# A two-layer graph attention kernel: another order of products, copies and side work where one block of queries follows the last

## The chip, the cores and the metric

The kernel runs on one NeuronCore of a Trainium2 chip. Five engines work side by side, each through its own list of instructions in order: TensorE (PE, matrix products into PSUM), VectorE (DVE), ScalarE (ACT, here almost only exponentials), GpSimd (POOL, which here works in SBUF alone) and SyncE (SP, which here only issues transfers). An instruction that must wait for another engine holds up everything behind it on its own engine. The metric is device time in microseconds (us) of one execution; lower is better.

## The reference

There are 3327 nodes with 128 features and a dense 0/1 matrix `adj` of 3327 x 3327. Cut to what matters:

```python
# layer 0: graph attention over the neighbours
H = x @ W.T + b;  s = H @ a_s;  r = H @ a_r
e = leaky_relu(A * s + A * r.T, 0.2)
x = layernorm(x + softmax(where(A > 0, e, NEG), axis=1) @ H)
# layer 1: attention in 128 slices of 8 channels, adj added twice to the scores
q = (x @ Wq.T).reshape(128, n, 8)      # k and v alike
a = softmax(einsum('dnh,dmh->dnm', q, k) * 128 ** -0.5 + adj + adj, axis=2)
out = einsum('dnm,dmh->dnh', a, v).reshape(n, 1024)
x = layernorm(x + out @ Wo.T)
```

Layer 1 is nearly all of the work: 128 matrices of 3327 x 3327 scores, each with its exponential, and products with only 8 channels on either side. The kernel takes no maximum in its softmax (a flag computed on the way tells whether that is safe, and a general program stands behind it for other inputs).

## The kernel before, in words

**The main loop (L1126 to L1187).** The 128 slices are taken in 32 groups of 4. The 3327 queries of a group are taken in 7 blocks of 476 (the last one a little narrower), and the 3327 keys in 26 tiles of up to 128. That makes 224 blocks. One block is 26 *rounds*, so there are 5824 rounds. A round makes the scores of one key tile for four slices, as two halves of two slices. For each half (128 keys x 2 x 476 queries):

- PE multiplies keys by queries (L152, `scb`) into a PSUM tile of two banks.
- The `adj` term gets in by one of two ways. In an *add* tile, DVE adds `adj` to the scores (L1175) and writes to SBUF, and ACT takes the exponential of both halves at once, 1904 wide, one round later (`exp_late`, L991: the *late* exponential). In a *times* tile, ACT takes the exponential straight from PSUM, 952 wide (L1172: the *direct* one), and POOL multiplies it by a factor 1 + (e^2 - 1) adj (L1173).
- PE multiplies the result `e` by the values (`products`, L950; the products are L956) and sums over the 26 key tiles in one PSUM bank `av`. After the last tile DVE copies `av` to SBUF (L966) and SP writes it out.

Key tiles come in threes: one times tile i and two add tiles i+1, i+2. `laid` (L927) writes out the three rounds of a three: direct half 1 of i with add half 0 of i+1; direct half 0 of i with add half 1 of i+1; both add halves of i+2. An even block has eight threes and then two rounds with tile 24 (times) and tile 25 (add). An odd block starts with one round of tile 25 (add), then eight threes (rounds 1 to 24), then a round in which tile 24 is half direct and half add. Even and odd blocks alternate. By *passage* I mean the last rounds of a block with the first rounds of the next.

**Buffers.** Scores for adds have two PSUM tiles (`pd`, L920), scores for direct exponentials one (`pe`, L921), `av` one (`pv`, L922), and the side work one bank.[...] `e` has seven SBUF tiles.

**When the products run.** `multiply` (L977) appends the round's tile to a list and, at the end of the round, runs products while more than `LAG` = 4 tiles wait: one tile's four products per round, four rounds after its turn. So a block's last products run at the end of round 3 of the next block, the copy of `av` follows on DVE, and the first products of the new block (round 4) wait for that copy. In odd blocks the products and copy of round 3 stand between the two adds of that round (`between`, L1162).

**Side work.** Layer 0 for the 26 tiles of rows, the projections to q, k and v, the counting of `adj` (L326, a part of the flag) and the results of layer 1 (`result`, L482) are cut into small pieces that run between rounds. A piece has a letter: `p` runs on PE at the head of a round (side products are L241, transposes L376 and L502), `d` on DVE at its end, `l` (the low halves, L409) on DVE as well, `m` on POOL (weights of layer 0: `weigh`, L308, and `mask`, L317), `x` issues transfers. Pieces wait in two rows, `main` and `aside`; `n` and `t` entries make a piece wait for a mark that another one sets. `lane` and `reading` (L1007 to L1017) say in which rounds a letter may run: `p`, `d` and `m` in round 0 and 25 of even blocks, in round 25 of odd ones, and in every third round between; `p` also in round 3 (4 in odd blocks). The counts stand in `aside`, behind the weights. `finish_to` (L1108) runs what is still missing when a new group needs its rows.

Of the kernel before, what the change touches and what calls it, by code (L numbers as in the profile page):

```python
# [17 lines left out]
P = 128  # L18
# [29 lines left out]
def kernel(  # L48
# [29 lines left out]
    H = wqT.shape[1]  # L78
# [71 lines left out]
    def special():  # L150
# [9 lines left out]
        with ExitStack() as sx, tc.manual_schedule(engines=ALL):  # L160
# [9 lines left out]
            CH = [(i, min(i + CW, NT)) for i in range(0, NT, CW)]  # L170
# [96 lines left out]
            def layer0(t, side=True, trow=None, bank=bank, held=None):  # L267
# [5 lines left out]
                s = {"a": {}, "w": {}}  # L273
                q0 = t * len(CH)
# [190 lines left out]
                for n, (i0, i1) in enumerate(CH):  # L465

                    aside.append(("n", ("P", q0 + n - 2, 0)))
                    for c0 in range(i0, i1, 3):
                        c1 = min(c0 + 3, i1)
                        aside.append(("m", lambda n=n, c0=c0, c1=c1: weigh(n, c0, c1)))  # L470
                        aside.append(("m", lambda n=n, c0=c0, c1=c1: mask(n, c0, c1)))
                    aside.append(("t", ("W", q0 + n)))
                    c = [("d", lambda n=n, h=h, k=k: count(n, h, k)) for h in range(3) for k in range(2)]
                    counts.append(c)
                    main.append(("n", ("W", q0 + n, 3)))
                    if i1 == NT:
                        main.append(("m", biased))
                    main += [("p", lambda i=i: product(i)) for i in range(i0, i1)] + [("t", ("P", q0 + n))]
                    aside.append(counts[-1])
                return loads, main + chain + [("t", ("rows", t))], aside  # L480

            def result(t):  # L482
# [440 lines left out]
            LAG = 4  # L923
# [90 lines left out]
            def lane(kind, n, odd):  # L1014

                if kind == "l":
                    return int(reading(n - 1, odd) if n else True)  # L1017
                return int(reading(n, odd) or kind == "p" and n - odd == 3)

            made = [layer0(t) for t in range(1, NT)]  # L1020
            first_loads = made[0][0]
            main = []
            aside = []
            for n, (_, m, a) in enumerate(made):

                later = []
                for u in a:
                    if u[0] == "r":

                        at = max((k for k, v in enumerate(aside) if v[0] == "n"), default=0)  # L1030
# [8 lines left out]
                if n == 0:  # L1039

                    for k, u in enumerate(later):
                        aside += u + [made[1][0][k]] * (len(made) > 1)
                main.append(m)
            main.append([("n", ("counts", 0, 0))] + judge())
            aside.append(("t", ("counts", 0)))
# [3 lines left out]
            side = {"main": [], "aside": aside, "since": {"main": 0, "aside": 0}, "read": -2}  # L1049

            def head(row, now, force=False):

                while True:
                    if not side[row]:
                        if row == "aside":
# [24 lines left out]

            def work_tensor(now, n, odd):

                for _ in range(lane("p", n, odd) if side["read"] != now - 1 else 0):
                    if head("main", now) != "p":
                        break
                    run("main", now)

            def work(now, n, odd):
                room, low, pool = lane("d", n, odd), lane("l", n, odd), lane("m", n, odd)
                for row in ("main", "aside"):  # L1090
                    while True:
                        kind = head(row, now)
                        if kind == "x":
# [13 lines left out]

            def finish_to(mark, now):  # L1108
                while mark not in marks:
                    row = "main" if head("main", -1 if now is None else now, True) else "aside"  # L1110
                    if head(row, -1 if now is None else now, True) is None:
                        break
                    run(row, -1)
                    tick(True)
# [13 lines left out]
            for g in range(NG):  # L1128
                k4, v4, _ = group
                for b in range(NBLK):  # L1130
# [5 lines left out]
                    for n, rnd in enumerate(rounds):  # L1136
# [437 lines left out]
```

## Time and profile before

| | |
|---|---|
| Time, median of 3 runs | 10047.45 us (10043.44 to 10048.37) |
| The profiled execution: time | 10052.42 us |
| The profiled execution: span of its instructions | 10050.6 us |
| Granted TensorE clock | 0.995 |
| ACT busy | 9897.6 us, 98% of the span |
| PE busy | 9477.4 us, 94% |
| DVE busy | 9188.5 us, 91% |
| POOL busy | 9177.2 us, 91% |
| DMA | mean 175 GB/s |

Times in the profile's timeline are microseconds from the start of the span. A timeline row has the start, the time over which the row's instructions ran, engine, line, operation, output<-input with shape and how many (x), and in brackets how long the engine was idle before and what ended that. "PEld" is the loading of weights for a product. The busy time of a matrix product is modelled, and instructions of one engine overlap in the records[...]. So the distance from one start to the next tells more of an engine's pace than the length of a row.

### The profile page before, as it was taken

Reading aid. Unit: us, or ns where it says so; the run is one execution under the profiler, and the core shown is the slowest. Engines: PE = TensorE matmul, PEld = TensorE weight load, DVE = VectorE, ACT = ScalarE, POOL = GpSimd, SP = SyncE. Lnnn points to the kernel's source line nnn. Section 1 sums busy time; section 2 is a strip of 40 time slices with the busy share of each in tenths; the row PEclk is TensorE's granted clock in tenths of the full one; section 3 lists DMA queues with packets and bytes.
Section 4 is the critical chain, followed back from the end, with each engine's and each line's share of the span. In section 5 each row is a group of like instructions: output and inputs, shape, how many; then the busy total and the mean of one; then the engine's idle time right before and its main releaser. Section 6 shows DMA issues by size and latency. Waiting matters only on the chain.

```text
span 10050.6 us, 207550 instructions
## 1 busy us (share of the span) xinstructions
PE 9477.4 (94%) x79523; PEld 3013.9 (30%) x79523; DVE 9188.5 (91%) x10554; ACT 9897.6 (98%) x7904; POOL 9177.2 (91%) x4954
## 2 busy tenths in 40 slices
PE   7999999999999999999999999999999999999998
PEld 2233333333233233323333333333333233222222
DVE  7899999999999999999999999999999999888888
ACT  7999999999999999999999999999999999999998
POOL 7999999999999999999999999999999999888887
PEclk9999999999999999999999999999999999999999
DMA  6765656665665656565566656566665565555554
GB/s 194 209 179 179 179 168 183 178 176 168 181 173 171 183 167 189 168 184 170 169 179 187 176 172 179 176 170 178 181 179 175 171 175 168 169 158 166 164 164 132
DMA packets 1399414, 1755.28 MB, mean 175 GB/s; under 512 B 349360, under 2 KB 1386890, under 8 KB 1394312
## 3 DMA queue, kind: packets, MB, share of 16 engines
q1 hardware_dynamic: 1388061, 1739.30, 59.7%
q8 instruction: 626, 10.26, 0.4%
q10 hardware_dynamic: 10347, 2.61, 0.1%
q14 instruction: 380, 3.11, 0.1%
HBM read 1637.49 MB, written 103.93 MB: 173 GB/s over the span
## 4 chain that ended last, share of the span: by engine, by line
ACT 41%; PE 21%; POOL 16%; issue 13%; DVE 7%; DMA 2%; SPq 1%; POOLq 0%; ACTq 0%; DVEq 0%
ACT e L991 29%; POOL e L1173 15%; ACT e L1172 11%; PE av L956 11%; PE scb L152 9%; DVE e L1175 5%; PE bank L241 1%; DVE o L966 1%; DMA q4b<-qT 1%; DMA at<-in_adjT_dram 1%; POOL w L308 0%; SPq L733 0%; POOL w L317 0%; DMA k4b<-kT 0%; POOL at L793 0%
## 5 line engine op out<-in xcount | busy, mean ns | idle before, releaser
L1173 POOL TENSOR_TENSOR e<-e,at 128x952 f32<-128x952 f32 (+1 forms) x3920 | 8715.9, 2236 | 788.6 <-ACT e L1172 735.1
L1175 DVE TENSOR_TENSOR e<-scb,at 128x952 f32<-128x952 f32 (+1 forms) x7728 | 8499.4, 1142 | 769.7 <-PE scb L152 650.1
L991 ACT ACTIVATE e<-e 128x1904 f32<-128x1904 f32 (+3 forms) x3920 | 7095.9, 1810 | 26.4 <-DVE e L1175 11.1
L956 PE MATMUL av<-e,v4b 128*32 128x476 f32 (+1 forms) x46592 | 5843.8, 573 | 99.0 <-DVE o L966 68.0
L152 PE MATMUL scb<-q4b,k4b 32*128 32x476 f32 (+1 forms) x23296 | 3882.4, 486 | 440.8 <-ACT e L1172 361.9
L1172 ACT ACTIVATE e<-scb 128x952 f32<-128x952 f32 (+1 forms) x3920 | 3921.1, 1000 | 74.9 <-PE scb L152 36.7
L152 PEld LDWEIGHTS scb<-q4b,k4b 32*128 32x128 f32 (+1 forms) x23296 | 1779.3, 189 | 5459.2 <-ACT e L1172 3161.5
L956 PEld LDWEIGHTS av<-e,v4b 128*32 128x32 f32 (+1 forms) x46592 | 1014.1, 109 | 1239.9 <-issue 933.4
L241 PE MATMUL bank<-hsb,w 128*32 128x129 f32 (+1 forms) x5200 | 278.6, 286 | 0.0
L326 DVE TENSOR_SCALAR_CACHE_REDUCE dump<-a 128x384 bf16<-128x384 f32 (+2 forms) x468 | 247.3, 528 | 0.6
L308 POOL TENSOR_SCALAR w<-trow,er 128x129 f32<-128x129 f32 x650 | 231.6, 376 | 1.3
L317 POOL TENSOR_TENSOR w<-w,a 128x384 f32<-128x384 f32 (+3 forms) x225 | 207.9, 924 | 0.1
L966 DVE COPY o<-av 128x476 f32<-128x476 f32 (+1 forms) x224 | 145.2, 648 | 31.3 <-PE av L956 30.4
L241 PEld LDWEIGHTS bank<-hsb,w 128*32 128x32 f32 (+1 forms) x5200 | 102.9, 108 | 148.2 <-issue 148.2
L241 PE MATMUL bank<-wo,ot 128*32 128x128 f32 x1600 | 85.2, 285 | 0.0
L402 DVE TENSOR_SCALAR hi<-bank 128x256 fp32r<-128x256 f32 (+1 forms) x200 | 83.0, 415 | 0.0
L409 DVE SCALAR_TENSOR_TENSOR lo<-bank,hi 128x256 fp32r<-128x256 f32 (+1 forms) x200 | 83.0, 415 | 0.0
L241 PE MATMUL bank<-wk,x1T 128*32 128x256 f32 x800 | 63.9, 391 | 0.0
L241 PE MATMUL bank<-wq,x1T 128*32 128x256 f32 x800 | 63.9, 391 | 0.0
L241 PE MATMUL bank<-wv,x1T 128*32 128x256 f32 x800 | 63.9, 391 | 0.0
L502 PE MATMUL bank<-ident,o 128*128 128x128 f32 x225 | 52.0, 304 | 0.0
L290 POOL MEMSET a<- 128x128 f32 (+1 forms) x25 | 5.2, 208 | 44.4 <-DVE dump L326 44.4
(123 smaller groups left out, 647.3 us busy)
## 6 DMA issues: line engine op xcount, KB each, us to landing
at<-in_adjT_dram SPq DMA_DIRECT2D x1536, 476.0 KB
at<-ftd SPq DMA_DIRECT2D x1674, 238.0 KB
at<-in_adjT_dram SPq DMA_DIRECT2D x256, 472.0 KB
at<-ftd SPq DMA_DIRECT2D x279, 236.0 KB
k4b<-kT SPq DMA_DIRECT2D x128, 415.9 KB
q4b<-qT SPq DMA_DIRECT2D x1528, 29.8 KB
at<-in_adjT_dram SPq DMA_DIRECT2D x192, 208.2 KB
at<-in_adjT_dram SPq DMA_DIRECT2D x150, 238.0 KB
```

The costliest lines, as they stand in the source:

```text
L152: nc.tensor.matmul(dst, k4[32 * j : 32 * j + H4, first_key(i) : first_key(i) + 2 * r - 1 : 2], q4[32 * j : 32 * j + H4, :nb], start=True, ...
L241: nc.tensor.matmul(dst[c0:c1], w[:, c0:c1], mov, **kw)
L308: nc.gpsimd.tensor_scalar(w, s["t"][:, :, :T3], -LOWEST, e, op0=ALU.min, op1=ALU.max)
L317: nc.gpsimd.tensor_tensor(w, w, s["a"][n][:, c0 - i0 : c1 - i0, :r], op=ALU.mult)
L326: nc.vector.tensor_scalar(z, a, float(k), None, op0=ALU.is_equal, op1=ALU.add, accum_out=even[:, t, at : at + 1])
L402: nc.vector.tensor_scalar(hi[:r, o : o + QW], s["b"][:r, :QW], scale, None, op0=ALU.mult)
L956: nc.tensor.matmul(s.av[32 * j : 32 * j + 32, : s.w], s.v4[:r, j, i * H1 : i * H1 + 32], e[:r, j, : s.w], start=(s.left == NT - 1), stop=( ...
L966: nc.vector.tensor_copy(o4[:, :w], s.av[:, :w])
L991: nc.scalar.activation(e, e, AF.Exp, scale=2.0)
L1172: nc.scalar.activation(eh, z[:r, :, :w], AF.Exp, scale=2.0)
L1173: nc.gpsimd.tensor_tensor(eh, eh, ah, op=ALU.mult)
L1175: nc.vector.tensor_tensor(eh, z[:r, :, :w], ah, op=ALU.add)
```

## The change

The change touches only the order of instructions; every matrix product, add and exponential is still there, on the same engine.

- `multiply` no longer follows one rule. In an even block's round 24 and an odd block's round 25 it runs the products of two tiles. From there until early in the next block three tiles wait instead of four, and then one round has no products (round 1 of an even block, round 5 of an odd one), after which four wait again. So after an even block, the last products and the copy of `av` come at the end of round 2 of the odd block (before: round 3). After an odd block they come at the end of round 3 of the even block, as before, but round 1 is empty and round 25 has two. `between` is gone: products always stand at the end of the round.
- `lane`: no side pieces in the passages, with two exceptions. In terms of the round within the eight threes, `p`, `d` and `m` have rounds 7, 10, ..., 22 and, of odd blocks, also round 25 of the block. A new letter `q` (side products of layer 0 and of the result's projection; `p` before) may also run one round before each of these, so two of them fit in a three. `l` has the round after.
- The counts of `adj`, with the loads of the next tile's `adj` behind them, form a third row, `counts`, and weights wait for these loads by a mark `L`.

```diff
@@ layer0
                     aside.append(("n", ("P", q0 + n - 2, 0)))
+                    aside.append(("n", ("L", q0 + n, 0)))
...
-                    main += [("p", lambda i=i: product(i)) for i in range(i0, i1)] + [("t", ("P", q0 + n))]
+                    main += [("q", lambda i=i: product(i)) for i in range(i0, i1)] + [("t", ("P", q0 + n))]
@@ result
-                units += [("p", lambda h=h: project(h)) for h in range(H)]
+                units += [("q", lambda h=h: project(h)) for h in range(H)]
@@ main loop
-            def multiply(s, i):
-                waiting.append((s, i))
-                while len(waiting) > LAG:
-                    products(*waiting.pop(0))
+            def multiply(n, odd):
+
+                k, lag = 1, LAG
+                if n == (NR - 1 if odd else NR - 2):
+                    k, lag = 2, LAG - 1
+                elif n < 5 if odd else n in (0, NR - 1):
+                    lag = LAG - 1
+                elif n == (5 if odd else 1):
+                    k = 0
+                for _ in range(k):
+                    if len(waiting) > lag:
+                        products(*waiting.pop(0))
...
-            def reading(n, odd):
-
-                n -= odd
-                if n % 3 == 1 and 4 <= n < NR - 2:
-                    return True
-                return n in ((NR - 2,) if odd else (0, NR - 1))
-
             def lane(kind, n, odd):
 
-                if kind == "l":
-                    return int(reading(n - 1, odd) if n else True)
-                return int(reading(n, odd) or kind == "p" and n - odd == 3)
+                n -= odd
+                if n == NR - 2 and odd:
+                    return int(kind != "l")
+                if n < 6 or n >= NR - 2:
+                    return int(kind == "l" and n == 0 and not odd)
+                return int(n % 3 == {"q": 0, "l": 2}.get(kind, 1) or n % 3 == 1 and kind == "q")
...
-            aside = []
+            aside, counts = [], []
...
                     elif isinstance(u, list):
-                        ahead = made[n + 1][0][sum(isinstance(v, list) for v in later)] if n + 1 < len(made) else None
-                        later.append(u)
-                        if n:
-                            aside += u + [ahead] * (ahead is not None)
+                        counts += u
+                        if n + 1 < len(made):
+                            counts += [("n", ("W", (n + 1) * len(CH) + k, 0)), made[n + 1][0][k], ("t", ("L", (n + 2) * len(CH) + k))]
+                        k += 1
...
             def work_tensor(now, n, odd):
 
-                for _ in range(lane("p", n, odd) if side["read"] != now - 1 else 0):
-                    if head("main", now) != "p":
-                        break
+                kind = head("main", now)
+                if kind in ("p", "q") and lane(kind, n, odd) and side["read"] != now - 1:
                     run("main", now)
...
-                for row in ("main", "aside"):
+                for row in ("main", "aside", "counts"):
...
                         work_tensor(g * total + at, n, odd)
-                        between = odd and n == LAG - 1
-                        for (i, h, at_) in rnd:
-                            if between and h == 1:
-                                multiply(s, order[n])
+                        for i, h, at_ in rnd:
...
-                        if not between:
-                            multiply(s, order[n])
+                        waiting.append((s, order[n]))
+                        multiply(n, odd)
                         work(g * total + at, n, odd)
```

More of the change, by code (lines that the diff above doesn't have):

```diff
@@ L1000, in special, with lane @@
             OPEN = min(18, total // 2)
-            def reading(n, odd):
+            def lane(kind, n, odd):
                 n -= odd
-                if n % 3 == 1 and 4 <= n < NR - 2:
-                    return True
-                return n in ((NR - 2,) if odd else (0, NR - 1))
-            def lane(kind, n, odd):
-                if kind == "l":
-                    return int(reading(n - 1, odd) if n else True)
-                return int(reading(n, odd) or kind == "p" and n - odd == 3)
+                if n == NR - 2 and odd:
[3 more added lines that the diff above has]
+                return int(n % 3 == {"q": 0, "l": 2}.get(kind, 1) or n % 3 == 1 and kind == "q")
             made = [layer0(t) for t in range(1, NT)]
@@ L1022, in special @@
             main = []
-            aside = []
+            aside, counts = [], []
             for n, (_, m, a) in enumerate(made):
-                later = []
+                k = 0
                 for u in a:
                     if u[0] == "r":
-                        at = max((k for k, v in enumerate(aside) if v[0] == "n"), default=0)
+                        at = max((k for k, v in enumerate(aside) if v[0] == "n" and v[1][0] == "P"), default=0)
                         aside.insert(at, ("x", u[1]))
                     elif isinstance(u, list):
-                        ahead = made[n + 1][0][sum(isinstance(v, list) for v in later)] if n + 1 < len(made) else None
-                        later.append(u)
-                        if n:
-                            aside += u + [ahead] * (ahead is not None)
+                        counts += u
+                        if n + 1 < len(made):
+                            counts += [("n", ("W", (n + 1) * len(CH) + k, 0)), made[n + 1][0][k], ("t", ("L", (n + 2) * len(CH) + k))]
+                        k += 1
                     else:
                         aside.append(u)
-                if n == 0:
-                    for k, u in enumerate(later):
-                        aside += u + [made[1][0][k]] * (len(made) > 1)
                 main.append(m)
             main.append([("n", ("counts", 0, 0))] + judge())
-            aside.append(("t", ("counts", 0)))
+            counts.append(("t", ("counts", 0)))
             results = [((needs[t] + 1) * total + LAG + 6, result(t)) for t in range(NT - 1)]
@@ L1048, in special @@
             marks = {("P", q): 0 for q in range(len(CH))}
-            side = {"main": [], "aside": aside, "since": {"main": 0, "aside": 0}, "read": -2}
+            marks.update({("L", len(CH) + k): 0 for k in range(len(CH))})
+            side = {"main": [], "aside": aside, "counts": counts, "since": {}, "read": -2}
             def head(row, now, force=False):
@@ L1054, in head @@
                     if not side[row]:
-                        if row == "aside":
+                        if row != "main":
                             return None
@@ L1109, in finish_to @@
                 while mark not in marks:
-                    row = "main" if head("main", -1 if now is None else now, True) else "aside"
-                    if head(row, -1 if now is None else now, True) is None:
+                    at = -1 if now is None else now
+                    row = next((row for row in ("main", "aside", "counts") if head(row, at, True)), None)
+                    if row is None:
                         break
```

## The prediction

> **What bounds the kernel now.** I read the page first: busy times, then the chain.
>
> ```profile
> PE 9477.4 (94%) x79523; PEld 3013.9 (30%) x79523; DVE 9188.5 (91%) x10554; ACT 9897.6 (98%) x7904; POOL 9177.2 (91%) x4954
> ACT 41%; PE 21%; POOL 16%; issue 13%; DVE 7%; DMA 2%; SPq 1%; POOLq 0%; ACTq 0%; DVEq 0%
> ```
>
> ACT is the bound, with three engines close behind it. By starts of ACT's 7840 exponentials in the trace, its pace between passages is fixed: 0.842 us from a direct exponential to the next instruction, 1.681 from a late one, 0.888 from a late half one (medians; durations are longer because records overlap). An even and an odd block have 35 direct, 34 late and one half: 35 x 0.842 + 34 x 1.681 + 0.888 = 87.5 us, and 112 pairs make 9801. The e-work runs from 66 to 10025 us, 9959. So 158 us are lost to stalls, and no reordering can gain more. Where they lie is seen in the timeline of the two passages (here blocks 99 to 101). First, odd to even:
>
> ```profile
> 4528.95 1.03 ACT L1172 ACTIVATE e<-scb 128x952 f32<-128x952 f32 x1
> 4529.79 1.07 ACT L991 ACTIVATE e<-e 128x952 f32<-128x952 f32 x1
> 4530.68 1.03 ACT L1172 ACTIVATE e<-scb 128x952 f32<-128x952 f32 x1
> 4531.52 1.87 ACT L991 ACTIVATE e<-e 128x1904 f32<-128x1904 f32 x1
> 4533.34 0.96 ACT L1172 ACTIVATE e<-scb 128x952 f32<-128x952 f32 x1
> 4534.22 1.79 ACT L991 ACTIVATE e<-e 128x1904 f32<-128x1904 f32 x1
> 4535.16 0.64 DVE L966 COPY o<-av 128x476 f32<-128x476 f32 x1
> 4535.85 0.16 PEld L956 LDWEIGHTS av<-e,v4b 128*32 128x32 f32 x8 [0.52 <-DVE o L966]
> 4535.92 0.94 ACT L1172 ACTIVATE e<-scb 128x952 f32<-128x952 f32 x1
> 4536.95 1.79 ACT L991 ACTIVATE e<-e 128x1904 f32<-128x1904 f32 x1
> 4538.87 0.97 ACT L1172 ACTIVATE e<-scb 128x952 f32<-128x952 f32 x1
> ```
>
> These ACT rows are rounds 0 to 6. Start to start, 4531.52 to 4533.34 is 1.82 where 1.68 is due, then 0.88 for 0.84, 1.70 for 1.68, 1.03 for 0.84 and 1.92 for 1.68: 0.63 late in all, though no gap stands in brackets. Median of all such passages: 0.68. Then even to odd (its ACT rows: round 4):
>
> ```profile
> 4578.62 0.65 DVE L966 COPY o<-av 128x476 f32<-128x476 f32 x1 [0.16 <-PE av L956]
> 4579.19 3.25 DVE L1175 TENSOR_TENSOR e<-scb,at 128x952 f32<-128x952 f32 x3
> 4579.27 1.08 ACT L1172 ACTIVATE e<-scb 128x952 f32<-128x952 f32 x1
> 4579.33 0.16 PEld L956 LDWEIGHTS av<-e,v4b 127*32 127x32 f32 x8 [0.62 <-DVE o L966]
> 4580.43 1.79 ACT L991 ACTIVATE e<-e 128x1904 f32<-128x1904 f32 x1
> ```
>
> Here the copy stands before the second add of round 3, and the late exponential waits for that add: 1.16 for 0.84, 0.32 late (median 0.33). Together 1.01 per pair, 113 us of the 158. The rest is the first eight blocks (some 30 us, where POOL also makes the 63 factors, L793, of 0.59 each) and a few stretches of products at half pace.
>
> [...] The bracketed waits of 0.52 and 0.62 for the copy agree: there is one `av` bank. But ACT's delay at 4533.34 comes before any copy, from a chain through PE and the single `pe` bank, so I go by the trace's chains, not by the buffer alone.
>
> **The change part by part.** I use these intervals, start to start, from the trace's rows: scores to the next PE work 0.425; a tile's products to the next scores 0.93; scores to their exponential 0.605, to their add 0.60; an exponential to the next scores in its bank 1.07; an add to the scores that reuse its bank 1.20; add to add 1.057; second add to its late exponential 1.235; last products to copy 1.07; copy to products 0.70, to add 0.56. Two tiles' products in a row occur only in the drain:
>
> ```profile
> 10021.31 2.58 PE L956 MATMUL av<-e,v4b 128*32 128x472 f32 x24
> ```
>
> Three tiles in 2.58, the last about 1.0 long: 0.79 from one to the next. I take 0.80 for the first of a pair; 0.93 bounds it above.
>
> *Odd to even.* Zero is the start of the direct exponential of odd round 25; the trace's medians then have that round's second score pair at -0.56. After the change, two tiles of products follow: -0.14 and 0.66, scores of round 0 at 1.59 (before: 1.10; needed by 2.52 - 0.6). Products 2.01, scores of round 1 at 2.94, and its direct half when its bank is free, 2.52 + 1.07 = 3.59. No products now. Adds: round 0 at 2.19, round 1 at 3.54. Scores of round 2: first pair 4.02, second pair 4.74, since it needs the bank of the add at 3.54. Products 5.17, scores of round 3 at 6.10, exponential 6.70; due 6.78 (before 6.94): in time. On DVE the adds of round 2 start at 4.62 and 5.68, of round 3 at 6.74; the last products at 6.52 allow the copy at 7.59, DVE takes it at 7.80. Scores of round 4 have their bank at 6.78 + 1.07 = 7.85, its add runs at 8.45, and the late exponential of round 5 may start at 9.69; due 10.14. The new `av` waits for the copy until 8.50; scores of round 5 at 9.43, products 9.86, scores of round 6 at 10.79, exponential 11.39; due 11.82. So nothing is lost, unless a side piece runs in round 25: by the order of the changed kernel 52 of 112 odd blocks have a PE piece there (about 39 of 0.24 to 0.26, 13 projections of 0.455) and 92 a DVE piece (0.33 to 0.54). They push round 3 past its due time by about 0.17 and 0.4. Mean loss with some for DVE: 0.16 instead of 0.68, times 112: **-58 us** (between -40, if the pair of products takes 0.93 + 0.93, and -70).
>
> *Even to odd.* Zero is the direct exponential of even round 24. That round's second score pair is at -0.80 to -0.43, later with side pieces in round 22; in the new order 98 of 112 have a DVE piece there and 69 a PE piece, so mostly -0.43. Products -0.01 and 0.79, scores of round 25 at 1.72 (before 1.10), the add of tile 25 at 2.32 (1.67). Its late exponential, first of the odd block, can start at 3.56; due 3.37. That is 0.19. Scores of odd round 0 need the same add's bank: 3.52; products 3.95, scores of round 1 at 4.88, exponential 5.48; due 5.05. So 0.43 late; from -0.80 it is 0.06; mean some 0.35. Later the copy, now after both adds of round 2 and before those of round 3, delays nothing: the late exponential that was 0.32 late has its add 0.35 early. So the stall moves from round 4 to rounds 0 and 1 and keeps its size: 0.35 for 0.33, **+2 us** (-25 to +25).
>
> *POOL.* Two multiplications take 2 x 2.19 of a three's 5.05 us and leave 0.67. A weight piece (1.05) or mask piece (0.92) adds 0.3 of backlog, a chunk's six about 1.9, and they come in consecutive threes. Before, the products of tile 24 ran at 8.4 and its POOL result was there at 5.9: slack 2.4, and backlog hid in it. Now they run in round 2, at about 7.0, slack 1.0, with the copy behind them on DVE, and the next products and scores on PE. In the new order 34 of 112 even blocks have a POOL piece in round 22, and with only 13 slots per pair (17 before) chunks follow each other closely. If the mean wait there is 0.8: 0.27 per odd passage, 0.05 per even one: **+36 us** (0 to +70).
>
> *Side rows.* The same pieces (3366) run in both; none are left over for the end, three run by force before group 1. In the threes one more side product of 0.24 fits: scores and products take 3 x 1.355 of 5.05. `adj` for a mask is loaded at least 22 rounds (some 38 us) before it. SP issues the same transfers in nearly the same places, those of the copy one round earlier in odd blocks. POOL's clearing of a new `adj` buffer (L290) stands right behind the DVE count that it waits for, as before. But in the first seven blocks, where POOL also makes factors, there are 32 weight pieces for 25: 7 x 0.9 and a little more: **+8 us** (0 to +15).
>
> Sum: -58 + 2 + 36 + 8 = -12 on the profiled 10052.4 us: 10040. The median of the runs is 5 us lower: **10036 us**. A measurement can tell about 0.2%, 20 us.
>
> **The rivals.**
> 1. *POOL's backlog stays hidden* (for: the waits view of before has little of it, most of it in the first blocks; against: slack falls from 2.4 to 1.0). Then -58 + 2 + 5 + 5: 10001, and 9985 if the odd passage too gets away.
>
> ```profile
> PEld av L956 <- POOL e L1173: 114.9, 358, 3.9
> ```
>
> 2. *Products moved forward wait for POOL*, slower: PE waits in rounds 25 to 2, and the copy, the new `av` and all scores wait behind it (for: the slack above; against: only a third of the passages meet a running chunk). I took 0.32 per pair; from 0.43 the gain is gone, from 0.6 the loss can be measured, at 0.8 (90 us for 36) it is 10090.
> 3. *The stall only moves* (for: ACT is due at the same moments and PE has the same work): gain of one passage lost in the other. This is close to my forecast; I count it with it.
>
> **How the numbers follow.** Forecast with 3: 0.47, own range 10015 to 10058. Rival 1: 0.33, 9975 to 10025. Rival 2: 0.20, 10060 to 10120. Range 9990 to 10080 leaves out about a tenth at each end. Faster by over 0.2% (below 10027): 0.36; within 0.2%: 0.45; slower (over 10067): 0.19.
>
> **What would show it.** ACT's start-to-start times in even rounds 2 to 6 near 1.68 and 0.84; in odd rounds 0 and 1 a late start, in round 4 none; PE's waits for POOL (the products' line is now L957) above the 114.9 us; the copy's waits gone or smaller. I am wrong if even rounds still stall, if odd round 1 is on time, or if stalls show between passages, where two side products now share a three.

## The result and the profile after

| | before | changed |
|---|---|---|
| Median of 18 runs each | 10047.53 us | 10063.33 us |
| Lowest and highest | 10043.44 to 10054.69 | 10056.29 to 10070.50 |
| Ratio, 95% interval | | 1.0016 (1.0009 to 1.0023) |
| Profiled execution | 10052.42 us | 10057.69 us |
| Its granted clock | 0.995 | 0.991 |

The change made the kernel 0.16% slower; the forecast was 10036, 0.1% faster. The page of the changed kernel, its busy times, clock row and chain:

```profile
PE 9430.8 (94%) x79523; PEld 2991.9 (30%) x79523; DVE 9188.1 (91%) x10554; ACT 9884.2 (98%) x7904; POOL 9179.8 (91%) x4954
PEclk8999999999999999999999999999999999999999
PE 40%; ACT 28%; POOL 16%; issue 9%; DVE 6%; DMA 2%; SPq 0%; POOLq 0%; DVEq 0%; ACTq 0%
```

The instructions are those of before, and the busy times nearly so (PE's lower by 0.5%, those of ACT, DVE and POOL within 0.2%). But PE's share of the chain has gone from 21% to 40%, and ACT's from 41% to 28%: ACT still has the most work, and more of the chain now runs through PE. The waits view (what waited for what; total us, times, longest) gives a first hint, before and then changed:

```profile
PEld av L956 <- DVE o L966: 127.9, 222, 1.1
PE av L956 <- POOL e L1173: 29.2, 36, 3.6
```

```profile
PEld av L957 <- POOL e L1172: 156.3, 313, 3.0
PE av L957 <- POOL e L1172: 74.4, 91, 2.7
PEld av L957 <- DVE o L967: 52.3, 111, 0.9
```

The weight loads' waits for the copy have fallen from 127.9 to 52.3 us. Those for POOL have grown from 114.9 to 156.3, and the products' own waits for POOL from 29.2 to 74.4.

**Where the time went.** As in the prediction I take the starts of ACT's exponentials and sum what lies above the pace of 0.842, 1.681 and 0.888 us. A delay in rounds 22 to 25 of one block or 0 to 11 of the next is put down to that passage. Blocks 8 to 223, and the first eight apart, in us:

| lost | before | changed | difference | forecast |
|---|---|---|---|---|
| 108 passages odd to even | 80.8 | 19.9 | -60.9 | -58, and +5 for POOL |
| 108 passages even to odd | 40.0 | 92.8 | +52.8 | +2, and +30 for POOL |
| between passages | -0.1 | 3.0 | +3.1 | 0 |
| first eight blocks | 34.9 | 46.7 | +11.8 | +8 |

Only one row is far from its forecast, the passage into odd blocks. First the other one, the passage into block 100 of the changed kernel (ACT's rows of the timeline: start, us, what):

```profile
4539.74 1.03 ACT L1171 ACTIVATE e<-scb 128x952 f32<-128x952 f32 x1
4540.58 1.08 ACT L1000 ACTIVATE e<-e 128x952 f32<-128x952 f32 x1
4541.47 1.04 ACT L1171 ACTIVATE e<-scb 128x952 f32<-128x952 f32 x1
4542.31 1.88 ACT L1000 ACTIVATE e<-e 128x1904 f32<-128x1904 f32 x1
4543.99 1.05 ACT L1171 ACTIVATE e<-scb 128x952 f32<-128x952 f32 x1
4544.84 1.89 ACT L1000 ACTIVATE e<-e 128x1904 f32<-128x1904 f32 x1
4546.52 1.06 ACT L1171 ACTIVATE e<-scb 128x952 f32<-128x952 f32 x1
4547.36 1.90 ACT L1000 ACTIVATE e<-e 128x1904 f32<-128x1904 f32 x1
4549.04 1.07 ACT L1171 ACTIVATE e<-scb 128x952 f32<-128x952 f32 x1
```

Start to start: 0.84, 0.89, 0.84, 1.68, 0.85, 1.68, 0.84, 1.68. Nothing is lost where the kernel before lost 0.63. Now the passage into odd block 103:

```profile
4670.02 1.22 ACT L1171 ACTIVATE e<-scb 128x952 f32<-128x952 f32 x1
4671.05 1.87 ACT L1000 ACTIVATE e<-e 127x1904 f32<-127x1904 f32 x1
4673.03 0.96 ACT L1171 ACTIVATE e<-scb 128x952 f32<-128x952 f32 x1
4673.89 1.78 ACT L1000 ACTIVATE e<-e 127x1904 f32<-127x1904 f32 x1
```

1.03 where 0.84 is due, then 1.98 where 1.68 is due: 0.19 late at the odd block's first late exponential, 0.49 in all one step later. The prediction's walk by hand had 0.19 and 0.43 at these two places. This passage is an undisturbed one. But 23 of the 108 lost 1.64 each on average (the part on the clock tells why), and the 14 in which POOL was latest 2.1 each.

### The profile page after: what moved, and what is told of

The parts are those of the page before. It is cut to its first block, busy times and chain, and to the rows that moved or that the text cites. A ratio compares the mean times of both kernels' runs of the same rounds, so it can differ in the third digit from the quotient of the medians.

```text
span 10055.9 us, 207766 instructions
## 1 busy us (share of the span) xinstructions
PE 9430.8 (94%) x79523; PEld 2991.9 (30%) x79523; DVE 9188.1 (91%) x10554; ACT 9884.2 (98%) x7904; POOL 9179.8 (91%) x4954
## 4 chain that ended last, share of the span: by engine, by line
PE 40%; ACT 28%; POOL 16%; issue 9%; DVE 6%; DMA 2%; SPq 0%; POOLq 0%; DVEq 0%; ACTq 0%
PE av L957 21%; ACT e L1000 19%; PE scb L152 15%; POOL e L1172 14%; ACT e L1171 9%; DVE e L1174 4%; PE bank L241 3%; POOL w L308 1%; POOL w L317 1%; DVE o L967 1%; DMA at<-in_adjT_dram 0%; DMA q4b<-qT 0%; DMA at<-ftd 0%; PE bank L503 0%; SPq L734 0%
## 5 line engine op out<-in xcount | busy, mean ns | idle before, releaser
L1000 ACT ACTIVATE e<-e 128x1904 f32<-128x1904 f32 (+3 forms) x3920 | 7196.6, 1836 | 5.1 <-DVE e L1174 4.0
L957 PE MATMUL av<-e,v4b 128*32 128x476 f32 (+1 forms) x46592 | 5820.4, 575 | 151.9 <-POOL e L1172 74.4
L152 PE MATMUL scb<-q4b,k4b 32*128 32x476 f32 (+1 forms) x23296 | 3828.4, 487 | 440.7 <-ACT e L1171 219.4
L1171 ACT ACTIVATE e<-scb 128x952 f32<-128x952 f32 (+1 forms) x3920 | 4025.2, 1027 | 116.4 <-PE scb L152 85.9
L152 PEld LDWEIGHTS scb<-q4b,k4b 32*128 32x128 f32 (+1 forms) x23296 | 1724.1, 190 | 5358.9 <-ACT e L1171 2909.9
L957 PEld LDWEIGHTS av<-e,v4b 128*32 128x32 f32 (+1 forms) x46592 | 1048.6, 109 | 1364.8 <-issue 905.5
L241 PEld LDWEIGHTS bank<-wo,ot 128*32 128x32 f32 x1600 | 31.5, 108 | 45.8 <-issue 45.8
```

The costliest lines, as they stand in the source:

```text
L152: nc.tensor.matmul(dst, k4[32 * j : 32 * j + H4, first_key(i) : first_key(i) + 2 * r - 1 : 2], q4[32 * j : 32 * j + H4, :nb], start=True, ...
L241: nc.tensor.matmul(dst[c0:c1], w[:, c0:c1], mov, **kw)
L957: nc.tensor.matmul(s.av[32 * j : 32 * j + 32, : s.w], s.v4[:r, j, i * H1 : i * H1 + 32], e[:r, j, : s.w], start=(s.left == NT - 1), stop=( ...
L1000: nc.scalar.activation(e, e, AF.Exp, scale=2.0)
L1171: nc.scalar.activation(eh, z[:r, :, :w], AF.Exp, scale=2.0)
```

## The experiments

Two theories stood at the start. T: the pair of products in even round 24 delays the odd block, so undoing the order of the even-to-odd passage brings the gain back. R: the side rows or the POOL work cost it, wherever the products stand. A third, C (the clock), came from the first traces. Ratios below are against runs of the kernel before on the same chip.

### One passage alone

The odd-to-even order alone, with the new side rows; after even blocks the old order with its `between` is kept:

```diff
-                if n == (NR - 1 if odd else NR - 2):
+                if odd and n == NR - 1:
                     k, lag = 2, LAG - 1
-                elif n < 5 if odd else n in (0, NR - 1):
+                elif not odd and n == 0:
                     lag = LAG - 1
-                elif n == (5 if odd else 1):
+                elif not odd and n == 1:
                     k = 0
```

> New order of products only where an odd block passes into an even one (two tiles' products in odd round 25, none in even round 1); where an even block passes into an odd one, products and copy as in the kernel before (one tile per round, the copy between the two adds of odd round 3). Side pieces and rows as in the changed kernel. Theory T (the pair of products in even round 24 delays the scores of round 25, and with them tile 25's add and the first exponential of the odd block): passages into even blocks lose about 20 us in all (81 before the change, 20 after), passages into odd ones about 40 (40 before, 93 after), the first eight blocks 5 to 12 more than before: 9985 to 10005 us. Theory R (the new places of the side pieces cause the odd passages' loss, whatever the products' order): passages into odd blocks still lose over 80 us: 10040 us or more.

10010.27 us, ratio 0.9962 (0.9948 to 0.9975). Lost into even blocks 19.8, into odd 44.7 (before 40.0). The losses are T's; the time is 5 us above T's range, since the first eight blocks lost some 12 us more than before, the top of what was allowed for them, and the odd passages 5. It is the fastest of all versions that leave no work out, and faster than both kernels. So the even half of the change is worth its forecast.

The even-to-odd order alone (the tests above with odd and even the other way round, so that odd blocks end as before):

> New order of products only where an even block passes into an odd one; into even blocks one tile per round as before. Side pieces and rows as in the changed kernel. T: passages into odd blocks lose about 93 us as in the changed kernel, into even ones 70 to 81: 10110 to 10130 us. R: the products' order matters little in the odd passages, and the rest is the same as under T here: 10100 to 10130; this run alone does not tell T from R, it shows whether the two passages' losses simply add.

10088.53 us, 1.0040 (1.0026 to 1.0054), below the range of both theories. Into even 74.9, near the 80.8 of the kernel before; into odd 66.5, not 93. So the losses of the two passages don't simply add. Only 9 odd passages of its trace show the disturbance by the clock that is told below, not 23. That the other engines get ahead of ACT where the even passage stalls, and so lose less in the odd one, is my reading; no run tests it.

### Side rows alone, products alone

New side rows with the old products and `between`:

> Products and copy in the order of the kernel before in both passages; side pieces and rows in the new places. T: passages into odd blocks lose 30 to 45 us, into even ones 65 to 80 (no side piece is left in even rounds 0 and 3), the first eight blocks some 10 more than before: 10040 to 10060 us. R: passages into odd blocks lose over 80: 10090 us or more.

10051.08 us, 1.0002 (0.9994 to 1.0011): into odd 34.7, into even 73.5, first eight blocks 46.4. The side rows cost 12 us in the first eight blocks and give as much back in the passages. New products with the old side rows (pieces in the passages again):

> Products and copy in the new order in both passages; side pieces and rows in the places of the kernel before (also in even rounds 0, 3, 4, 25 and odd 4, 5). T: passages into odd blocks lose 75 to 100 us, into even ones 25 to 50 since pieces stand in rounds 0, 3 and 4: 10045 to 10080 us. R: passages into odd blocks lose 40, as before: 9990 to 10020 us.

10073.28 us, 1.0025 (1.0018 to 1.0032): into even 75.5, so the gain there is gone, which T's 25 to 50 did not have. The empty passages are what the pair in round 25 needs, and 18 even passages now show half clock (the next part tells of it). Into odd about 69: 35 with the rows alone, 69 with the products alone, 93 with both. So R falls, and the odd passage's products are the cause; but some 24 of the 93 come up only together with the side rows. Here too, as with the even-to-odd order alone, the even passages stall and few odd ones (7) show half clock.

### The clock

The traces' records of the granted clock hold stretches at half rate (the record's value is 0.5), of 3.41 us in these two kernels' passages from block 8 on (the changed one has four of 6.83 before that). From block 8 on the kernel before has 6 in its passages, all beginning 1.3 to 1.7 us after an even block's first exponential; the changed one has 23 in odd passages, 16 of them beginning 10.0 to 10.5 us after the odd block's first exponential. There round 5 has no products. One of them, in block 51 of the changed kernel, in the windows view (window, its length, then busy us and instructions of PE, PEld, DVE, ACT, POOL; clock; DMA share; GB/s) and in PE's and ACT's timeline:

```profile
2373.40:2376.90 3.50, 2.22 (x20) 0.74 (x16) 3.22 (x4) 3.50 (x4) 3.15 (x2) 0.99 0.93 297
2376.90:2380.30 3.40, 3.40 (x26) 1.08 (x28) 2.36 (x3) 2.63 (x3) 2.26 (x2) 0.51 0.33 115
```

```profile
2374.73 0.84 PE L152 MATMUL scb<-q4b,k4b 32*128 32x476 f32 x6
2376.51 0.52 PE L152 MATMUL scb<-q4b,k4b 32*128 32x476 f32 x2 [0.94 <-DVE e L1174]
2376.96 1.81 PE L957 MATMUL av<-e,v4b 128*32 128x476 f32 x8
```

```profile
2377.00 1.81 ACT L1000 ACTIVATE e<-e 128x1904 f32<-128x1904 f32 x1
2379.57 0.96 ACT L1171 ACTIVATE e<-scb 128x952 f32<-128x952 f32 x1 [0.77 <-PE scb L152]
```

PE waits 0.94 us for an add, with no products to run meanwhile. In the next window the clock is 0.51, one tile's products take 1.81 us where they took 1.00 (at 2373.80 in the same block), and the exponential comes 2.57 after the last instead of 1.68. To test whether PE's gap is the cause, three score pairs are repeated in odd rounds 5 and 6, which write the same result again:

```diff
+                            for t in [0, 1] * ((z is None) if odd and n == 5 else 2 * (h == 0) if odd and n == 6 else 0):
+                                pair_scores(sc[i, h][: kr[i], t, :w], s.k4, s.q4, i, kr[i], 2 * h + t, w)
```

> The changed kernel, with three pairs of score products made again in odd rounds 5 and 6 (once for the direct half of round 5, twice for the first half of round 6; the same values into the same bank), 0.42 us each, where PE otherwise stands idle for up to 1.4 us since round 5 has no products of values. The output is the same. Theory C (that idle stretch makes the granted clock fall to one half for 3.41 us in 22 of the 108 odd passages of the trace, which costs some 0.75 us each): the half-clock stretches in odd passages go to 0 to 4, passages into odd blocks lose 70 to 78 us for 93: 10040 to 10052 us. Rival P (the stretches are an effect of passages that are late for another reason, such as POOL): they stay near 20, and the time stays at 10058 to 10070.

10044.10 us, 0.9994 (0.9986 to 1.0002): 19 us less than the changed kernel (22 by the ratios, as the kernel before took 10050.8 beside it), by added work. Stretches in odd passages fall from 23 to 1, the loss into odd blocks from 92.8 to 77.4.

One thing could give the same figures without the fill. The stretches begin on a fixed grid of 3.41 us (the last section), and where its points fall differs from trace to trace: in the changed kernel 28 fell 10.0 to 10.5 us after an odd block's first exponential, and 16 of them began a stretch; in this one 13 fell there, and none did. In block 51 of this kernel none fell there at all. So here is a passage of it with a point there (into block 215, the point at 9635.10), in windows on either side of the point:

```profile
9631.70:9635.10 3.40, 2.52 (x26) 1.10 (x22) 2.98 (x4) 3.40 (x4) 3.05 (x2) 1.00 0.87 282
9635.10:9638.50 3.40, 3.21 (x30) 0.90 (x34) 3.08 (x3) 3.40 (x4) 2.81 (x3) 1.00 0.36 128
```

26 matrix products in the first window instead of 20, and the clock stays at 1.00 in the second. PE's wait for the add is still there, but 0.64 us instead of 0.94. All 18 runs of the changed kernel have a mean clock of 0.989 to 0.991, all 13 of this one 0.994 or 0.995, so it isn't the luck of one trace. C holds here.

### Other places for the pair

If T is right, an earlier or later pair should help. First, no side pieces in even round 22, so that its scores come early:

```diff
+                if n == NR - 4 and not odd:
+                    return 0
```

> The changed kernel without side pieces in round 22 of even blocks (they move to later rounds; nothing is left out). Theory T: the second score pair of even round 24 then comes 0.2 to 0.35 us earlier, and so do the scores of round 25, the add of tile 25 and the first direct exponential of the odd block, which is late by 0.1 to 0.25 instead of 0.49; POOL has less backlog there: passages into odd blocks lose 40 to 65 us for 93, in all 10015 to 10045. Rival: the pair of products sets the delay alone, whatever stands in round 22: 10055 us or more.

10072.70 us, 1.0022 (1.0013 to 1.0031). In passages without a half-clock stretch the loss fell to 0.46 (changed kernel: 0.65), but 35 passages had one, at 1.47 each, and the first eight blocks lost 5 us more. The time is the rival's; the step that T put ahead of it did get smaller. Then the pair one round later, in even round 25:

```diff
...
+                elif not odd and n == NR - 1:
+                    k, lag = 2, LAG - 1
...
```

> Into even blocks as in the changed kernel. Into odd blocks the two tiles' products stand in even round 25 instead of round 24 (from there three wait, and odd round 5 is empty, as in the changed kernel). T: the add of tile 25 is no longer late (1.7 after the direct exponential of round 24, not 2.27), and the first direct exponential of the odd block is late by about 0.15 instead of 0.49; POOL's backlog and the half-clock stretches stay: passages into odd blocks lose 45 to 70 us, in all 10010 to 10035. Rival (moving a product forward costs the same wherever it stands): 10055 us or more.

10060.03 us, 1.0011 (1.0004 to 1.0017): 0.62 without a stretch, and 24 with one. The add of tile 25 was on time (1.76 us after the direct exponential of round 24, in the median), but the next steps lost as before. This is the rival's time, not T's. Then the pair in odd round 1, with the empty round at 3 instead of 5:

```diff
...
+                elif odd and n == 1:
+                    k, lag = 2, LAG - 1
+                elif odd and n == 2:
+                    lag = LAG - 1
+                elif odd and n == 3:
+                    k = 0
...
```

> Into even blocks as in the changed kernel. Into odd blocks the two tiles' products stand in odd round 1, so the last ones still come in round 2 and the copy after that round's adds; round 3 has no products. T: nothing ahead of round 1 is delayed, the scores of round 2 by 0.3 where 0.6 are free; the late exponential and the direct one of round 4 are on time: passages into odd blocks lose 10 us, and with POOL's backlog (its result for tile 24 is needed about 1 us after it is there) 20 to 35: 9975 to 10000 us. Rival C (an empty round 3 lets the clock fall as the empty round 5 did): 10005 to 10025.

10093.18 us, 1.0043 (1.0030 to 1.0057), the slowest of all, and above both ranges: 59 passages with a stretch, 1.70 each. In those without, the loss is 0.29, below the 0.37 of the kernel before. As an order it is the best of the three; the clock spoils it. If that is so, filling its gap should turn it round. First try, the pair of the first half of round 3 repeated:

```diff
+                            for t in [0, 1] * (2 * (odd and n == 3 and h == 0)):
+                                pair_scores(sc[i, h][: kr[i], t, :w], s.k4, s.q4, i, kr[i], 2 * h + t, w)
```

> The pair of products for the odd passage stands in round 1 of the odd block, round 3 is empty, and PE's gap there is filled by repeating the score pair of the first half of round 3 twice (the same result is written again). The kernel without the fill lost 0.29 in passages without a half-clock stretch and 1.70 in the 59 with one. Theory C (half-clock stretches follow PE's gap): at most 8 stretches, loss into odd blocks 28 to 45 us, time 9996 to 10012, at or below the kernel with the even passage's products alone (10010). Rival (the loss there is one of the order itself): 40 or more stretches or a loss above 80 us, time over 10050.

10073.14 us, 1.0024 (1.0015 to 1.0034): 35 stretches, loss into odd 102.8. By loss and time this is what the rival said. PE's timeline in block 55, first without a fill, then with this one, tells why:

```profile
2554.85 1.11 PE L152 MATMUL scb<-q4b,k4b 32*128 32x472 f32 x6
2556.86 0.49 PE L152 MATMUL scb<-q4b,k4b 32*128 32x472 f32 x2 [0.90 <-DVE e L1180]
```

```profile
2554.64 1.12 PE L152 MATMUL scb<-q4b,k4b 32*128 32x472 f32 x10
2556.87 0.49 PE L152 MATMUL scb<-q4b,k4b 32*128 32x472 f32 x2 [1.11 <-DVE e L1182]
```

Ten matrix products of scores stand in 1.12 us where six stood in 1.11: the repeats ran ahead of the gap, which is still there (1.11 and 0.90). So three score pairs were put into the gap itself, into the free bank of the direct exponential:

```diff
+                            if odd and n == 3 and h == 1:
+                                fill = pe.tile([P, 2, 512], F32, name="scb")
+                                for t in [0, 1] * 3:
+                                    pair_scores(fill[: kr[i], t, :w], s.k4, s.q4, i, kr[i], t, w)
```

> As the kernel filled in round 3 (10073), but the repeats now stand where PE's gap is: three score pairs more, between the two score pairs of odd round 3, into the bank of the direct exponential, which is free there; nobody reads them. In the kernel filled before, matmul starts fell to 0.7 per 0.5 us between 5.5 and 6.5 us into the odd block, as in the one without a fill, and all but two half-clock stretches came in the passages where the 3.41 us grid has a point from 7 to 8.5. Theory C (stretches follow that gap): at most 5 stretches, loss into odd blocks 30 to 45 us, time 9996 to 10014. Rival (this order loses by itself, the stretches follow from late exponentials): 25 or more stretches, time over 10050.

```profile
2543.58 2.50 PE L152 MATMUL scb<-q4b,k4b 32*128 32x472 f32 x14
```

10021.47 us, 0.9974 (0.9963 to 0.9984). The gap is gone: one row of 14 without a wait. Stretches in odd passages fall from 59 to 4, and the time by 72 us against the same order without a fill (about 70 by the ratios); the mean clock is 0.980 to 0.982 in the five runs without a fill, 0.993 or 0.994 in these nine. So C holds here too, and the rival falls. The loss into odd blocks is 56.8, above the 30 to 45 that I expected, and the time 7 us above its range: 14 passages with a late POOL still lose 2.16 each, 30 us of it.

### POOL's weights

In the filled kernel (from here on the changed kernel with the first fill, 10044.1 us) the passages can be sorted by when POOL finished tile 24, counted from the direct exponential of even round 24. Where it was done by 6.2 us (73 of 107), the loss is 0.46; where it took over 8 us (14), it is 2.1. In the kernel before, POOL was never later than 8. Here is the passage into block 53 of the changed kernel, without any half-clock stretch:

```profile
2455.02 1.13 POOL L308 TENSOR_SCALAR w<-trow,er 128x129 f32<-128x129 f32 x3
2455.17 1.00 PE L957 MATMUL av<-e,v4b 128*32 128x476 f32 x8 [0.92 <-POOL e L1172]
2458.05 0.97 ACT L1171 ACTIVATE e<-scb 128x952 f32<-128x952 f32 x1 [0.62 <-PE scb L152]
2460.58 1.01 PE L957 MATMUL av<-e,v4b 128*32 128x476 f32 x8 [0.81 <-POOL e L1172]
2463.99 0.96 ACT L1171 ACTIVATE e<-scb 128x952 f32<-128x952 f32 x1 [0.65 <-PE scb L152]
```

Products wait 0.92 and 0.81 for POOL, and ACT then 0.62 and 0.65 for scores queued on PE behind them. Three kernels leave POOL's weight and mask pieces out for all tiles of rows but the first; a fixed tile of ones stands in for them, so layer 0 gives those rows a plain mean:

```diff
...
+                    if side:
+                        s["w"][n] = wfix
+                        return
                     for i in range(c0, c1):
                         w, e = s["w"][n][:, i - i0, :r], er[:, i : i + 1]
...
                 def mask(n, c0, c1):
+                    return
```

The filled kernel without weights:

> The filled kernel (10044), with POOL's weight and mask pieces of layer 0 left out for all tiles of rows but the first; the products of layer 0 take a fixed tile of ones instead, so those tiles get a plain mean over all rows in place of the attention of layer 0. Everything else is the same work. In the filled kernel's trace the loss into odd blocks is 0.46 where POOL finished tile 24 by 6.2 us and 2.1 in the 14 of 108 passages where it finished after 8. Theory P (POOL's backlog costs what the forecast put on it, about 0.27 per odd passage): loss into odd blocks from 77 to 46 to 54 us, first eight blocks from 47 to about 38, time 10003 to 10015. Rival (POOL is late there because ACT was late, not the other way round): loss into odd blocks stays above 70, only the first blocks gain, time 10030 to 10038.

9980.47 us, 0.9932 (0.9919 to 0.9946). Into odd 77.4 to 50.0, as P had it; the time is lower than P's 10003, because the first eight blocks went to 14.9, not 38, and into even from 23.6 to 14.8. The changed kernel without weights:

> The changed kernel with the same pieces left out (the attention of layer 0 becomes a plain mean for all tiles of rows but the first). Theory (half-clock stretches come from PE's own gap in odd rounds 4 to 6 and not from POOL): 15 to 30 odd passages still show one, and the time lies 13 to 25 us over the filled kernel without weights: 10018 to 10035. Rival (backlog on POOL empties PE and brings the half-clock stretches): at most 8 such passages, time within 8 us of the filled kernel without weights.

10013.46 us, 0.9967 (0.9954 to 0.9979); the first eight blocks, again mis-sized by me (46.7 to 13.5), put it below the range. 35 odd passages have a half-clock stretch (1.44 each, 0.47 in the others), more than the 15 to 30 expected. So POOL doesn't bring the stretches, and the 35 explain the 33 us to the filled kernel without weights: 35 x (1.44 - 0.47) = 34. They also hide most of the gain: into odd blocks this kernel loses 84, only 9 less than with weights. The kernel before without weights:

> The kernel before with the same pieces left out (the attention of layer 0 becomes a plain mean for all tiles of rows but the first). Forecast's view: its slack of 2.4 us hides POOL's backlog between blocks, so loss into odd blocks stays at 38 to 42 and into even ones at 76 to 82; only the first eight blocks gain, some 10 of 35 us: time 10035 to 10042. Rival (the pieces on POOL cost the same in both kernels): gain as large as in the changed kernel, 10010 to 10022.

10025.09 us, 0.9977 (0.9968 to 0.9986). The time is between the two ranges, but the trace decides: into odd 40.9 (40.0 with weights), into even 78.8 (80.8), first eight blocks 14.0 (34.9). In the old order the weights cost nothing between blocks, only at the start.

## Why the prediction was right and wrong

**Odd to even: right.** With weights the loss fell by 60.9 us; without, it is 78.8 before and 14.8 in the filled kernel: -64, forecast -58 (-40 to -70). The second tile of the pair in round 24 started 0.82 after the first, 0.80 assumed.

**POOL: right.** Forecast 30 into odd, 5 into even. Weights cost 27.4 into odd in the filled kernel and nothing before; into even 8.8 and 2.0. Rival 1, POOL hidden, is out. Rival 2 has the measured 10063 in its range (10060 to 10120), but by luck: it needed POOL at 0.6 or more per pair, and the weights cost (27.4 + 8.8) / 108 = 0.34, the forecast's 0.32.

**Side rows: right in kind, somewhat low.** +11.8 in the first eight blocks for +8; without weights the two kernels are equal there (13.5 and 14.0), so it is the weights beside the factors, as it said.

**Even to odd: the step that failed.** "So the stall moves from round 4 to rounds 0 and 1 and keeps its size: 0.35 for 0.33, +2 us." The place was right: before, undisturbed odd passages lose 0.33 at the late exponential of round 4; in the filled kernel without weights they lose 0.14 at round 0's late one and 0.28 at the direct one of round 1, the walk's 0.43 in all, and nothing in round 4. Two things were wrong. First its size: without weights and stretches it is 0.46 against 0.38 per passage (50.0 against 40.9 in 108), +9 us. The walk had 0.43 for the usual case, and block 103 shows it; I averaged in a piece-less case of 0.06, with the scores of round 24 at -0.80, that hardly occurs: in nine of ten passages they came after -0.65. Second, and larger, a term that the sum didn't have at all: the empty round 5 leaves PE a gap, and the half-clock stretches that follow it cost 15 us in the profiled executions (92.8 to 77.4) and 19 in the medians (10063.3 to 10044.1). They were in reach: the prediction lists "a few stretches of products at half pace" in the kernel before, and asked neither what they follow nor what a round without products does to PE. With POOL's 27 us these two make up nearly all of the 52.8 us in the table's second row: 9 + 27 + 15. How much falls to POOL and how much to the clock depends on which goes first: without weights the same fill takes 34 us off the odd passages (84 to 50), not 15.

**The sum.** The measured 10063 lies above the forecast's own range (10015 to 10058), inside the wide one (9990 to 10080), and on the wrong side of the kernel before. With the gap filled the changed kernel takes 10044.1; the forecast was 10036. So the missing term is the whole of the slowdown: with it gone, the interval of the ratio (0.9986 to 1.0002) no longer tells the kernel from the one before, and a gain isn't shown. The term also spreads the runs: of the changed kernel's 18, the seven with a mean clock of 0.991 average 10059.8 us, the seven with 0.990 10064.3, the four with 0.989 10070.0. One thousandth of 10056 us is 10 us of clock, by my estimate some six stretches (3.41 us at half rate are 1.71 us of clock each), and six times the 1 us that one costs a passage (1.64 for 0.65) is about what the steps show (4.5 and 5.7). The profiled execution, at 0.991, is one of the shorter ones, and that of the kernel before, at 10052.4, one of its longer ones, so the +5.3 us between them understates the medians' +15.8, and the table of losses with it.

**Rival 3** ("the stall only moves") describes the undisturbed odd passage well, and was counted with the forecast. What it did not have is that the new place also exposes POOL and the clock.

## What to carry to other kernels

When an order of work is made by hand, look at what the engine that gets an empty round does in it. A bound on one engine (ACT here) says nothing of a second one: here PE, left with gaps of about 1 us, had its clock at half rate for 3.41 us in 23 of 108 passages, and in 1 with the first fill. Judge the two halves of a change apart; here one is worth 38 us (10048.5 to 10010.3), and the other takes it all back and 16 more. And measure stalls by the distance from start to start: where records overlap, the brackets mislead. They have ACT's direct exponentials waiting 36.7 us for scores before and 85.9 after, where the starts show 155.6 and 162.4 us lost in all.

## What was not expected of the hardware

The half-clock stretches begin on a fixed grid: in the clock records of the changed kernel's trace, the starts of the 26 after 500 us all lie within 0.01 us of one grid, and its period, fitted to these starts, is 3.4133 us. Most (16 of the 23 in the changed kernel's odd passages) came where a grid point fell just behind PE's gap. In the changed kernel without weights 33 grid points fell 10.0 to 10.5 us after the start of an odd block, and 32 began a stretch; of all others from 1 us before to 14 us after the start, three did. With the gap filled and no weights 18 fell there, and none began one. PE was far from idle before them: in the 3.41 us before each of the 24 stretches that the changed kernel has in passages from block 8 on, 8 to 20 matrix products began, with a median of 16, where the median of the other grid intervals is 26. In block 51 PE was busy for 2.22 of the 3.50 us before its stretch, and its longest gap, just ahead of the grid point, was 0.94 us.

What exactly decides stays open. In the changed kernel itself only 16 of the 28 points at that place began a stretch, and some 200 of its other grid intervals also had 20 products or fewer and no stretch followed. Neither the count nor the length of the one gap separates them: PE's wait of 1.25 us that ended at 7240.79, right at a grid point, was followed by a clock of 1.00, and the stretch at 9063.56 came after waits of 0.41, 0.41 and 0.56 us.
